# One-hot weights on ScalarE, chunks of other sizes, t added by TensorE for 16 of 18 tiles, and last loads in rows of 4 KB

## The chip, the cores and the metric

One Trainium2 chip, one NeuronCore. The time is the device time of one execution in microseconds (us), and the number that counts is the median of several runs. One execution is also taken with the hardware profiler; its span and its rows are what the sections below read. Engines: TensorE (PE in the profile; PEld is its weight load), VectorE (DVE), ScalarE (ACT), GpSimd (POOL) and SyncE (SP, which here only issues DMAs).

## The reference, cut to what matters

Input x is 1x256x48x48 (2304 tokens of 256 channels), all in float32.

- Layer 0: group norm, then an attention in which the four heads are folded into the tokens (9216 rows of 64), and x is added. This is the large part.
- Layer 1, attention over slices: tokens t are normalised, a softmax `sw` over 64 slices is computed per token, tokens are gathered into slices, 8 heads attend among the 64 slices, and the result is spread back with `sw` and added to t:

```python
denom = jnp.sum(sw, axis=1)[:, None, :, None] + 1e-09
qs = jnp.einsum('bhnd,bns->bhsd', q, sw) / denom      # ks, vs likewise
tok = jnp.einsum('bhst,bhtd->bhsd', attn, vs)
out = jnp.einsum('bhsd,bns->bnhd', tok, sw).reshape(b, n, H * D)
return out @ Wout + bout                               # t = t + this
```

- Layer 1, experts: t is normalised, a gate takes the best 2 of 8 experts for every token, and t gets the weighted sum of `gelu(t @ W1[e]) @ W2[e]` of the two.
- The output is t turned back to 1x256x48x48.

## The kernel before, in words

The tokens lie as 18 tiles of 128 (`NTT = 18`). `t_sb` holds all 18 in SBUF, each with 256 channels and 8 gate logits (`C + E = 264`).

Layer 0's attention runs from the start to about 1235 us in a loop over 18 query blocks by 36 key pairs; the change leaves it alone. Its small steps for layer 1 (`out_proj`, `turn`, `slices`, `gather`) run beside it, so that at its end `sw`, its transposes `swT` and the sums over tokens (`ts_sum`, `den`, `pts`) are ready.

Most engine calls go through the wrappers `pe`, `dve`, `act`, `pool` (class `InOrder`, line 49; its call is line 57, so most groups of the profile have that line). These calls stay in the order in which they are written. Calls on `nc.…` directly may be moved by the scheduler of the language; the gathers and scatters of the experts (lines 1082 and 1142) are such calls on POOL. DMAs marked SPq are issued by SP in its own order.

What follows the attention, in order:

1. **Attention among the slices** (lines 730 to 854, tiles `ph`, `psc`, `pv`, `pa`, `pk`, `pw`, ending with `tw`). One chain of small matmuls and VectorE steps. Between them `busy(n, spin)` issues n matmuls of 128x256 whose output nobody reads.
2. **Tiles** (lines 857 to 905). For each tile TensorE multiplies `swT` by `tw` into a PSUM bank `py` (the two 64-row halves of a transposed tile serve two tiles). For even tiles VectorE adds t from SBUF and takes the statistics (`bn_stats`, `bn_aggr`); for odd tiles TensorE adds t by a matmul with the identity, VectorE takes the statistics from PSUM, and ScalarE copies the sum to `t_sb`. The tiles come in groups of 6, 6, 4 and 2. At the end of a group POOL computes `rstd_t` and `shift`, SP writes `t_d` (the running t in DRAM), and the function `normed` of the group before lets ScalarE write the normalised rows to `tn2` (a ring of two buffers) and SP write them to `tn_d` in DRAM.
3. **Gate and routing** (lines 917 to 991). VectorE finds the two best experts per token (`lg`, `sel`) and the place of each token in its expert's list (`pos`, `slot`). TensorE counts with `pto` and `pin`; ScalarE computes the exponential `e2` and then loads the table of Gelu.
4. **One-hot stage** (lines 995 to 1055). The list of tokens per expert tile comes from one sum of matmuls. For each of the 36 (choice, tile) pairs j, `what[:, j]` holds two rows of 43 numbers (the one-hot `in_tile` times the token number, and times its weight), `in_row[:, j]` a one-hot of 128; TensorE sums `in_row` times `what` over j into `pw`. `in_row` lies on `t_sb`'s memory. The work is done in four chunks of 9, `in_tile` in two of 18, and `find_experts` (between the chunks) gives the expert of each tile:

```python
for k in range(0, K, G):                 # K = 36, G = 9
    ks = slice(k, k + G)
    if k % NTT == 0:
        find_tile(k, NTT)
    dve.tensor_tensor(what[:, ks], in_tile[:, ks, :]..., wkf[:, ks, :]..., ALU.mult)
    dve.tensor_tensor(in_row[:, ks, :], bc(row[:, ks], ...), back..., ALU.is_equal)
    if k == 0:
        find_experts()
```

   Four VectorE instructions read `pw` (`empties`, `slot_t`, `slot_w`), and 14 spins run meanwhile.
5. **Experts** (lines 1057 to 1194). 36 tiles of 128 tokens always, up to 7 more behind tests. A tile's rows come by an indirect DMA from `tn_d` (`xs`, two buffers; the rows of the last seven tiles go to `late_xs`), W1 comes by SP (two buffers), TensorE turns the rows (`pt`), multiplies (`ph`), ScalarE applies Gelu (`hid`), TensorE multiplies by W2 in SBUF (`py`), and POOL scatters with addition into `t_d`.
6. **Tail**, `to_columns` (line 1213). SP loads t from `t_d` in five blocks of up to 512 tokens, TensorE transposes, VectorE copies the first 128 channels from PSUM to `ob` (three buffers) and ScalarE the others, SP writes the output.

Of the kernel before, what the change touches and what calls it, by code (L numbers as in the profile page):

```python
# [9 lines left out]
FP = mybir.dt.float32  # L10
AF = mybir.ActivationFunctionType
# [51 lines left out]
def layers(  # L63
# [430 lines left out]
    def attention():  # L494
# [180 lines left out]
        [P, 256], FP, name="spin"  # L675
    )
    ps_den = sums_done.enter_context(tc.tile_pool(name="ps_den", bufs=1, space=PSUM))
    ps_o = tail.enter_context(tc.tile_pool(name="ps_o", bufs=5, space=PSUM))
    den = ps_den.tile([P, S], FP, name="den")
    pts = ps_den.tile([P, 2, 2 * S], FP, name="pts")  # L680

# [47 lines left out]

    with tc.tile_pool(name="sa", bufs=1) as sa:  # L730
        tw = sa.tile([P, C + E], FP, name="tw")
        with sums_done, tc.tile_pool(name="ps_b", bufs=3, space=PSUM) as ps_b, tc.tile_pool(
            name="ps_sc", bufs=1, space=PSUM
        ) as ps_sc:

# [5 lines left out]
            for m in range(2):  # L741
                for c in range(2):
# [3 lines left out]
                    )  # L746
            busy(1, spin)
            rd = sa.tile([P, S], FP, name="rd")
            dve.tensor_scalar(rd, den, 1e-9, None, ALU.add)
            dve.reciprocal(rd, rd)  # L750
            dr = sa.tile([P, S], FP, name="dr")
            dve.tensor_mul(dr, den, rd)

            def times_dr(b, n):
# [32 lines left out]

            psc = ps_sc.tile([P, 2, 512], FP, name="psc")
            for u in range(2):
# [21 lines left out]
            act.activation(a, a, AF.Exp, scale=float(D1) ** -0.5)  # L811
            act.copy(vs, pv)
            aT = sa.tile([S, 2, 2, P], FP, name="aT")
            for v in range(2):
# [5 lines left out]
                else:  # L820
                    act.copy(aT[:, v], pa)
            busy(1, spin)
            dve.tensor_reduce(am, a, AX.X, ALU.add)
# [46 lines left out]
        shift = const.tile([P, NTT], FP, name="shift")  # L870
        with tc.tile_pool(name="ps_y0", bufs=7, space=PSUM) as ps_y0, tc.tile_pool(
            name="norm", bufs=2
        ) as norm:
            groups = [(0, 6), (6, 6), (12, 4), (16, 2)]
            for g, (i0, n) in enumerate(groups):
                pys = [ps_y0.tile([P, C + E], FP, name="py", tag="py") for _ in range(n)]
                for k, py in enumerate(pys):
                    j, u = divmod(i0 + k, 2)
                    rows = slice(u * S, (u + 1) * S)
                    pe.matmul(py, swT[rows, j, :], tw[rows, :], start=True, stop=(u == 0))  # L880
                for k in range(1, n, 2):
                    pe.matmul(pys[k], ident, t_sb[:, i0 + k, :], start=False, stop=True)
                for k, py in enumerate(pys):
                    i = i0 + k
                    s6 = small.tile([P, 6], FP, name="s6", tag="s6")
                    if k % 2 == 0:
                        dve.tensor_tensor(t_sb[:, i, :], t_sb[:, i, :], py, ALU.add)
                        dve.bn_stats(s6, t_sb[:, i, 0:C])
                    else:
                        dve.bn_stats(s6, py[:, 0:C])  # L890
                        act.copy(t_sb[:, i, :], py)
                    dve.bn_aggr(stats[:, i, :], s6)
                these = slice(i0, i0 + n)
                ve = small.tile([P, n], FP, name="ve6", tag="ve6")
                dve.tensor_scalar(ve, stats[:, these, 1], 1e-5, None, ALU.add)
                pool.tensor_tensor(rstd_t[:, these], ve, mhalf[:, 0:n], ALU.pow)
                pool.tensor_tensor(shift[:, these], stats[:, these, 0], rstd_t[:, these], ALU.mult)
                pool.tensor_scalar(shift[:, these], shift[:, these], -1.0, None, ALU.mult)
                nc.sync.dma_start(
                    out=t_d[i0 * P : (i0 + n) * P, :].rearrange("(i p) c -> p i c", p=P),  # L900
                    in_=t_sb[:, these, 0:C],
                )
                if g > 0:
                    normed(*groups[g - 1])
            normed(*groups[-1])

# [7 lines left out]
    with gating, tc.tile_pool(name="onehot", bufs=1) as oh, tc.tile_pool(  # L914
# [84 lines left out]
        in_tile = oh.tile([P, K, NSL], FP, name="in_tile")  # L999
        what_flat = oh.tile([P, K * 2 * NSL], FP, name="what")  # L1000
        what = what_flat.rearrange("p (k w n) -> p k w n", k=K, w=2)
        in_row = t_flat[:, 0 : K * P].rearrange("p (k r) -> p k r", r=P)
        pwide = ps_lg.tile([P, P], FP, name="pw")
        pw = pwide[:, 0 : 2 * NSL].rearrange("p (w n) -> p w n", w=2)
        busy(7, spin)
        G = 9
        wkf = wk.rearrange("p k i w -> p (k i) w")

        def find_tile(k, n):
# [4 lines left out]
            )  # L1014

        past = gp.tile([1, NSL, E - 1], FP, name="past")

        def find_experts():

            dve.tensor_tensor(  # L1020
                past, bc(steps[0:1, 0:NSL], [1, NSL, E - 1]),
                ends[0:1, 0 : E - 1].unsqueeze(1).to_broadcast([1, NSL, E - 1]), ALU.is_ge,
            )
            ex = gp.tile([1, NSL], FP, name="ex")
            dve.tensor_reduce(ex, past, AX.X, ALU.add)
            dve.tensor_copy(expert_i, ex)
            dve.tensor_copy(used_i, ends[0:1, E - 1 : E])

        for k in range(0, K, G):
            ks = slice(k, k + G)  # L1030
            if k % NTT == 0:
                find_tile(k, NTT)
            dve.tensor_tensor(
                what[:, ks], in_tile[:, ks, :].unsqueeze(2).to_broadcast([P, G, 2, NSL]),
                wkf[:, ks, :].unsqueeze(3).to_broadcast([P, G, 2, NSL]), ALU.mult,
            )
            dve.tensor_tensor(
                in_row[:, ks, :], bc(row[:, ks], [P, G, P]),
                back.unsqueeze(1).to_broadcast([P, G, P]), ALU.is_equal,
            )  # L1040
            if k == 0:
                find_experts()
        for j in range(K):
            n = 2 * NSL if j % G == G - 1 else P
            pe.matmul(
                pwide[:, 0:n], in_row[:, j, :], what_flat[:, j * 2 * NSL : j * 2 * NSL + n],
                start=(j == 0), stop=(j == K - 1),
            )
        busy(14, spin)

# [13 lines left out]
    with tc.tile_pool(name="ps_h", bufs=1, space=PSUM) as ps_h, tc.tile_pool(  # L1064
# [16 lines left out]
        def rows(s, xs):  # L1081
            nc.gpsimd.indirect_dma_start(  # L1082
                out=xs, out_offset=None, in_=tn_d[:, :],
                in_offset=bass.IndirectOffsetOnAxis(ap=slot_t[:, s : s + 1], axis=0),
                bounds_check=NT + P - 1, oob_is_err=True,
            )
            return xs
# [36 lines left out]
        def second(s, hid, meanwhile):  # L1124

            e = expert_of(s, mybir.EngineType.PE)
            py = next(ring_py)
            for f in range(NHC):
                pe.matmul(
                    py, hid[:, f, :],  # L1130
                    w2_sb[:, bass.ds(e, 1), f, :].rearrange("p e d -> p (e d)"),
                    start=(f == 0), stop=(f == NHC - 1),
                )
                if f == 2:
                    meanwhile()
            e = expert_of(s, mybir.EngineType.DVE)
            y = next(ring_y)
            dve.tensor_tensor(
                y, py, b2_e[:, bass.ds(e, 1), :].rearrange("p e d -> p (e d)"), ALU.add
            )  # L1140
            dve.tensor_scalar(y, y, slot_w[:, s : s + 1], None, ALU.mult)
            nc.gpsimd.indirect_dma_start(  # L1142
                out=t_d[:, :], out_offset=bass.IndirectOffsetOnAxis(ap=slot_t[:, s : s + 1], axis=0),
                in_=y, in_offset=None, bounds_check=NT + P - 1, oob_is_err=True,
                compute_op=ALU.add,
            )
# [51 lines left out]
def kernel(ctx: ExitStack, tc: tile.TileContext, *args):  # L1198
# [9 lines left out]

    again = nc.values_load(
        bad, min_val=0, max_val=1, skip_runtime_bounds_check_because="it is the result of a comparison"  # L1210
    )

    def to_columns():

        sp = InOrder(tc, nc.sync)
        with tc.tile_pool(name="fin", bufs=1) as fin, tc.tile_pool(name="fin3", bufs=3) as fin3, tc.tile_pool(
# [3 lines left out]
            for (t0, n), tt in zip(TBLOCKS, tts):  # L1220
                sp.dma_start(out=tt, in_=t_d[t0 : t0 + n, :].rearrange("(i p) c -> p i c", p=P))
            for (t0, n), tt in zip(TBLOCKS, tts):
                ob = fin3.tile([P, 2, 512], FP, name="ob", tag="ob")
                for c in range(2):
                    pt = ps_f.tile([P, 512], FP, name="pt", tag="pt")
                    for k in range(n // P):
                        nc.tensor.transpose(  # L1227
                            pt[:, k * P : (k + 1) * P], tt[:, k, c * P : (c + 1) * P], ident
                        )
                    if c == 0:  # L1230
                        nc.vector.tensor_copy(ob[:, c, 0:n], pt[:, 0:n])  # L1231
                    else:
                        nc.scalar.copy(ob[:, c, 0:n], pt[:, 0:n])  # L1233
                sp.dma_start(out=out_v[:, :, t0 : t0 + n], in_=ob[:, :, 0:n])
# [40 lines left out]
```

## Time and profile before

| | us |
|---|---|
| median of 3 runs | 1622.19 |
| the 3 runs | 1619.83, 1622.56, 1622.19 |
| the profiled execution's own time | 1621.32 |
| its span | 1619.3 |
| attention among the slices, from the sums to `tw` | 1250 to 1261.5 |
| tiles, first product to `lg` times `rstd_t` | 1261.56 to 1279.69 |
| one-hot stage, `in_tile` to the last product | 1289.10 to 1303.1 |
| first gather of rows, first `pt` | 1304.94, 1309.09 |
| last scatter issued, first load of the tail issued | 1596.09, 1600.19 |

Busy shares of the span: PE 97%, PEld 49%, DVE 65%, ACT 50%, POOL 9%. The page cuts the span in 40 slices of 40.5 us and gives the busy share of each in tenths:

```
PE   7999999999999999999999999999999699999995
PEclk9999999999999999999999999999999899999997
DMA  4000000000000000000000000000003756666665
```

PE and the clock granted to it are full nearly everywhere; the slices that differ are the first, the two around 1260 to 1340 us, and the last. In the timeline each row is a start, a duration, the engine, the line, the operation with output and inputs, the number of instructions merged (a float32 matmul gives two), and in brackets how long the engine was idle before and what ended that. A line "L57" is the wrapper's, so one goes by the names of the tiles.

### The profile page before, as it was taken

To read this page: it belongs to the slowest core of one execution; us is meant where nothing else is said; L and a number is where in the kernel's file an instruction comes from. 1 tells how busy PE (TensorE), PEld (TensorE's weight loads), DVE (VectorE), ACT (ScalarE), POOL (GpSimd) and SP (SyncE) were. 2 spreads that over 40 slices of the span, in tenths; PEclk is the share of its full clock that TensorE was granted. 3 is DMA by queue.
4 is the path that set the end of the run, shared out by engine and by line. 5 is a ranking of instruction groups with operands and counts; after the bars stand their busy time and mean duration, and the time that the engine had idled before them with its cause. 6 is when DMAs were issued, how large, how long until landed. Compare 5 with 4: busy or idle time off the path is not lost. (4 is left out here: it accounts for less than half of the span.)

```text
span 1619.3 us, 31854 instructions
## 1 busy us (share of the span) xinstructions
PE 1569.0 (97%) x13230; PEld 786.1 (49%) x13230; DVE 1046.2 (65%) x1369; ACT 810.8 (50%) x1100; POOL 140.3 (9%) x128
## 2 busy tenths in 40 slices
PE   7999999999999999999999999999999699999995
PEld 3633343333333333333333333333335489999995
DVE  7577778777787877877878778778687721111111
ACT  2365555555555655556556555565553322333321
POOL 0000000000000000000000000000000143333321
PEclk9999999999999999999999999999999899999997
DMA  4000000000000000000000000000003756666665
GB/s 137 1 1 1 1 1 1 1 1 1 1 1 1 2 1 1 1 1 2 1 1 1 1 1 1 1 1 1 1 2 98 253 182 189 178 181 190 173 157 181
DMA packets 39910, 79.26 MB, mean 49 GB/s; under 512 B 3613, under 2 KB 26218, under 8 KB 39626
## 3 DMA queue, kind: packets, MB, share of 16 engines
q1 hardware_dynamic: 32074, 66.35, 12.3%
q0 software_dynamic: 7680, 10.75, 3.8%
q8 instruction: 108, 1.77, 0.5%
q14 instruction: 48, 0.39, 0.1%
HBM read 64.64 MB, written 12.45 MB: 48 GB/s over the span
## 5 line engine op out<-in xcount | busy, mean ns | idle before, releaser
L57 DVE TENSOR_TENSOR acc<-acc,p 128x1024 f32<-128x1024 f32 x612 | 748.2, 1222 | 251.6 <-ACT p L57 243.5
L57 ACT ACTIVATE p<-s 128x1024 f32<-128x1024 f32 x648 | 662.9, 1023 | 490.0 <-PE s L57 479.8
L57 PE MATMUL av<-p,v_sb 64*64 64x512 f32 x5184 | 675.4, 590 | 1.0 <-DVE up L57 0.7
L57 PE MATMUL s<-q,kk 64*64 64x512 f32 x5184 | 676.2, 591 | 0.0
L57 PEld LDWEIGHTS s<-q,kk 64*64 64x64 f32 x5184 | 201.6, 133 | 352.6 <-issue 181.7
L57 PEld LDWEIGHTS av<-p,v_sb 64*64 64x64 f32 x5184 | 195.6, 131 | 358.3 <-ACT p L57 202.5
L57 ACT ACTIVATE hid<-ph,bcol 128x128 f32<-128x128 f32 x312 | 89.3, 368 | 216.9 <-PE ph L57 216.2
L57 PE MATMUL py<-w_sb,hid 128*128 x624 | 147.3, 379 | 0.0
L57 PEld LDWEIGHTS ph<-xT,w 128*128 128x128 f32 x1248 | 145.3, 192 | 2.7 <-DVE xT L57 0.8
L57 PE MATMUL ph<-xT,w 128*128 128x128 f32 x1248 | 145.7, 275 | 0.5 <-DVE xT L57 0.5
L57 POOL TENSOR_TENSOR rstd_t<-ve,mhalf 128x1 f32<-128x1 f32 (+3 forms) x22 | 28.0, 1271 | 1234.1 <-DVE ve L57 1234.1
L57 DVE COPY xT<-pt 128x256 f32<-128x256 f32 x40 | 17.0, 425 | 173.3 <-PE pt L57 173.3
L57 PEld LDWEIGHTS py<-w_sb,hid 128*128 128x128 f32 x624 | 112.7, 190 | 12.2
L1142 POOL DMA_INDIRECT t_d<-y,slot_t x39 | 61.7, 1583 | 98.7 <-DVE y L57 86.2
L57 DVE TENSOR_TENSOR y<-py,b_bc 128x256 f32<-128x256 f32 x39 | 16.6, 425 | 68.6 <-PE py L57 68.6
L1082 POOL DMA_INDIRECT xs<-tn_d,slot_t x36 | 38.4, 1065 | 110.6 <-PE pt L57 83.8
L57 DVE RECIPROCAL rinv<-pb 128x256 f32<-128x256 f32 x18 | 31.5, 1751 | 0.0
L57 DVE TENSOR_TENSOR acc<-p 128x1024 f32<-128x1024 f32 x18 | 22.1, 1225 | 9.9 <-ACT p L57 9.9
L314 DVE TENSOR_SCALAR q<-pp,bcol 64x512 f32<-64x512 f32 (+1 forms) x30 | 20.8, 694 | 7.4 <-PE pp L297 7.1
L57 DVE TENSOR_REDUCE up<-av 128x512 f32<-128x1024 f32 x18 | 21.9, 1217 | 0.0
L319 ACT ACTIVATE kk<-pp,bcol 128x512 f32<-128x512 f32 (+1 forms) x10 | 6.4, 644 | 21.8 <-PE pp L301 21.8
L297 PE MATMUL pp<-t_sb,WqT 128*128 128x512 f32 (+1 forms) x40 | 17.2, 553 | 0.0
(260 smaller groups left out, 602.0 us busy)
## 6 DMA issues: line engine op xcount, KB each, us to landing
w<-in_L_ffn_W_dram SPq DMA_DIRECT2D x40, 1024.0 KB, 5.6
w_sb<-in_L_ffn_W_dram SPq DMA_DIRECT2D x8, 1024.0 KB, 13.1
x_sb<-in_x_dram SPq DMA_DIRECT2D x4, 576.0 KB
t<-t_d SPq DMA_DIRECT2D x4, 512.0 KB, 6.9
out_dram<-ob SPq DMA_DIRECT2D x4, 512.0 KB
t_d<-t_sb SPq DMA_DIRECT2D x2, 768.0 KB, 3.6
tn_d<-tn SPq DMA_DIRECT2D x2, 768.0 KB, 3.7
b_bc<-in_L_ffn_b_dram SPq DMA_DIRECT2D x1, 1024.0 KB
```

The lines of the kernel that those rows point to most:

```text
L57: return self.tc.keep_in_program_order(getattr(self.engine, name)(*args, **kwargs))
L297: nc.tensor.matmul(pq[:, 0:tn], WqT[:, c, cols], xn[:, c, toks], start=(c == 0), stop=(c == 1))
L314: nc.vector.tensor_scalar(dst, pq[rows, 0:tn], bcol[rows, B_Q + m : B_Q + m + 1], 0.125, ALU.add, ALU.mult,)
L319: nc.scalar.activation(kk[:, m, toks], pk[:, 0:tn], AF.Identity, bias=bk_m)
L1082: nc.gpsimd.indirect_dma_start(out=xs, out_offset=None, in_=tn_d[:, :], in_offset=bass.IndirectOffsetOnAxis(ap=slot_t[:, s : s + 1], axis= ...
L1142: nc.gpsimd.indirect_dma_start(out=t_d[:, :], out_offset=bass.IndirectOffsetOnAxis(ap=slot_t[:, s : s + 1], axis=0), in_=y, in_offset=None ...
```

## The change

In the slices' attention the two PSUM banks of `den` and `pts` and the two of `psc` are made full banks. As soon as each has been read for the last time, TensorE puts a tile of t there by a matmul with the identity (tiles 0 to 3, in place of two spins); the later product with `tw` adds to it. For the other tiles TensorE adds t after the product, except for tiles 4 and 6, where VectorE still adds. Seven banks are used in turn. Group 0 is normalised after group 1's tiles, the others after all tiles.

```diff
+        def token_sums(i):
+            pe.matmul(banks[i][:, 0 : C + E], ident, t_sb[:, i, :], start=True, stop=False)
...
-            busy(1, spin)
...
+            for i in range(2):
+                token_sums(i)
...
+            token_sums(2)
             aT = sa.tile([S, 2, 2, P], FP, name="aT")
...
-            busy(1, spin)
+            token_sums(3)
...
+            banks = cycle(banks + [ps_y0.tile([P, 512], FP, name=f"py{k}") for k in range(3)])
+            by_dve = (4, 6)
...
+                for i in range(i0, i0 + n, 2):
+                    two = range(i, i + 2)
+                    for u, k in enumerate(two):
+                        rows = slice(u * S, (u + 1) * S)
+                        pe.matmul(
+                            pys[k - i0], swT[rows, i // 2, :], tw[rows, :], start=(k >= 4),
+                            stop=(k < 4 or k in by_dve),
+                        )
+                    for k in two:
+                        if k >= 4 and k not in by_dve:
+                            pe.matmul(pys[k - i0], ident, t_sb[:, k, :], start=False, stop=True)
...
-                    if k % 2 == 0:
+                    if i in by_dve:
...
-                if g > 0:
-                    normed(*groups[g - 1])
-            normed(*groups[-1])
+                if g == 1:
+                    normed(*groups[0])
+            for group in groups[1:]:
+                normed(*group)
```

In the one-hot stage ScalarE computes the weight rows, one instruction for each j; VectorE computes the token rows. The chunks are 3, 6, 9, 9, 6, 3, `in_tile` is made in 9, 9 and 18, and TensorE's products follow each chunk. The experts of the tiles are counted with the tile number on the partitions (7 numbers instead of 301) and turned by TensorE (`pex`). After it 9 spins, not 14.

```diff
+            for j in range(k, k + n):
+                act.activation(what[:, j, 1], in_tile[:, j, :], AF.Copy, scale=wkf[:, j, 1:2])
...
+            past = gp.tile([P, E - 1], FP, name="past")
+            dve.tensor_scalar(past, ends[:, 0 : E - 1], token1[:, 0:1], None, ALU.is_lt)
+            ex = gp.tile([P, 1], FP, name="ex")
+            dve.tensor_reduce(ex, past, AX.X, ALU.add)
+            pex = ps_lg.tile([1, P], FP, name="pex")
+            pe.transpose(pex, ex, ident)
...
+        for n in (3, 6, 9, 9, 6, 3):
+            ks = slice(k, k + n)
+            if k == 9:
+                dve.tensor_copy(expert_i, pex[:, 0:NSL])
+                find_tile(9, 9)
+            elif k == 18:
+                find_tile(18, 18)
+            dve.tensor_tensor(what[:, ks, 0], in_tile[:, ks, :], bc(wkf[:, ks, 0], [P, n, NSL]), ALU.mult)
...
-        busy(14, spin)
+        busy(9, spin)
```

The gathers and scatters of the experts, and the load of the flag `again`, are kept in program order:

```diff
-            nc.gpsimd.indirect_dma_start(
+            pool.indirect_dma_start(
                 out=xs, out_offset=None, in_=tn_d[:, :],
...
-            nc.gpsimd.indirect_dma_start(
+            pool.indirect_dma_start(
                 out=t_d[:, :], out_offset=bass.IndirectOffsetOnAxis(ap=slot_t[:, s : s + 1], axis=0),
...
+    for flag in flags:
+        tc.keep_in_program_order(flag)
```

In the tail a partition loads four consecutive tokens (two in the last block), that is 4 KB in one row instead of four rows of 1 KB. The transposed tokens then come out in another order, and the copies to `ob` restore it by writing with a step of four numbers:

```diff
-                sp.dma_start(out=tt, in_=t_d[t0 : t0 + n, :].rearrange("(i p) c -> p i c", p=P))
+                sp.dma_start(out=tt, in_=t_d[t0 : t0 + n, :].rearrange("(p i) c -> p i c", p=P))
...
+                    dst = ob[:, c, 0:n].rearrange("q (p k) -> q k p", p=P)
+                    src = pt[:, 0:n].rearrange("q (k p) -> q k p", p=P)
                     if c == 0:
-                        nc.vector.tensor_copy(ob[:, c, 0:n], pt[:, 0:n])
+                        nc.vector.tensor_copy(dst, src)
                     else:
-                        nc.scalar.copy(ob[:, c, 0:n], pt[:, 0:n])
+                        nc.scalar.copy(dst, src)
```

## Prediction

> **What bounds the kernel now.** I read the page first. Its line by slices shows TensorE at 97% and DMA idle through the attention, and a stretch near 1240 to 1310 us where TensorE dips. Neither attention nor the expert loop is touched, so I then took the merged timeline of 1241 to 1345 us, the waits of TensorE in the expert loop, and the chain that ended last for the tail. Between `tw` (1261.07) and the first gather of rows (1304.94) TensorE does not set the time: a chain of VectorE, ScalarE and DMA does.
>
> First, the timeline of the tiles: start, duration, engine, operation, and in brackets idle time and its releaser.
> ```profile
> 1261.07 0.43 DVE L57 TENSOR_TENSOR tw<-pw,bout_bc 128x264 f32<-128x264 f32 x1 [1.25 <-PE pw L57]
> ...
> 1265.40 0.40 DVE L57 BATCH_NORM_STATS2 s<-py 128x6 f32<-128x256 f32 x1
> 1265.83 0.38 ACT L57 COPY t_sb<-py 128x264 f32<-128x264 f32 x1 [1.09 <-DVE s L57]
> 1265.84 0.18 DVE L57 BATCH_NORM_AGGREGATE stats<-s 128x2 f32<-128x6 f32 x1
> 1265.93 0.40 DVE L57 TENSOR_TENSOR t_sb<-t_sb,py 128x264 f32<-128x264 f32 x1
> ...
> 1279.69 0.31 DVE L57 TENSOR_TENSOR lg<-lg,rstd_t 128x144 f32<-128x144 f32 x1
> ```
> The reader is to see that a tile summed by TensorE costs VectorE 0.53 us (1265.40 to 1265.93), and that ScalarE's copy starts only when the statistics are read.
>
> Second, the timeline from the norms to the one-hot stage.
> ```profile
> 1283.19 1.09 ACT L57 ACTIVATE tn<-t_sb,shift,rstd_t 128x256 f32<-128x256 f32 x2 [1.80 <-DMA tn_d<-tn]
> ...
> 1284.31 0.36 SPq L865 DMA_DIRECT2D tn_d<-tn  x1
> ...
> 1289.10 0.97 DVE L57 TENSOR_TENSOR in_tile<-first_slot,at_big 128x774 f32<-128x774 f32 x1
> ```
> The last two norms wait for a write of `tn_d`: the ring `tn2` has two buffers.
>
> Third, the timeline from the last one-hot matmuls to the third tile of the experts.
> ```profile
> 1299.53 1.35 DVE L57 TENSOR_TENSOR t_sb<-row,back 128x1152 f32<-128x1152 f32 x1
> 1299.79 3.39 PE L57 MATMUL pw<-what,t_sb 128*128 128x128 f32 x28
> ...
> 1303.01 6.24 PE L57 MATMUL spin<-Wqkv_sb,ident 128*128 128x256 f32 x28
> 1303.21 0.26 DVE L57 TENSOR_SCALAR empties<-pw,spare 128x43 f32<-128x43 f32 x1 [2.33 <-PE pw L57]
> ...
> 1304.94 1.33 POOL L1082 DMA_INDIRECT xs<-tn_d,slot_t  x1 [25.83 <-DVE slot_w L57]
> ...
> 1317.10 1.01 POOL L1082 DMA_INDIRECT xs<-tn_d,slot_t  x1 [0.30 <-issue]
> ...
> 1320.43 0.44 PE L57 MATMUL pt<-ident,xs 128*128 128x128 f32 x2 [1.52 <-DMA xs<-tn_d,slot_t]
> ```
> VectorE ends at 1300.88 and then waits 2.33 for nine matmuls; the third tile's gather is the tenth on POOL's queue, and TensorE idles 1.52 for it. After that TensorE runs through to 1595, so what is won before 1320 is won at the end.
>
> **Step 1, slices' attention: +0.4.** Four additions of t (128x264; six passes took 1.60, so about 0.47 for a sum of two passes) replace two spins (0.45 each, from 14 in 6.24). The first two fill a gap of TensorE (the products with `hsT` start at 1252.67, two sums from 1251.70 end at 1252.65): 0 to 0.1. The third waits for VectorE's last read of `psc` (1256.39) and is queued ahead of `pa`, which started at 1256.96; `pv`'s last passes end near 1256.85, so `pa` slips to about 1257.3: +0.35. The fourth takes a spin's place. Cover gone altogether: +1.0.
>
> **Step 2, the tiles: -2.6.** VectorE now has 16 tiles at 0.53 and two (4 and 6) at 0.99 (add 0.43, statistics 0.56), 10.5 in place of 15.25 (1262.37 to 1277.62). TensorE needs 0.48 for a pair of products and 0.47 for each of 12 sums, 10.0: it keeps up. But the gain is cut. The two halves of `psc` are one tile, and in the built order the statistics of its second half wait for ScalarE's copy of its first (tiles 3, 10, 17). Tile 17's does so behind ScalarE's six norms of group 0 (3.06), which start after copy 11. Counting from the first product: copy 11 ends at 9.4, norms at 12.5, copies 12 to 16 at 13.8, statistics 14.3, copy 17 at 14.7, POOL's `rstd_t` for two tiles (0.72) at 15.4, `lg` times `rstd_t` at 15.5. Before, it stood at 18.1 (1261.56 to 1279.69). Bounds: 13 without those waits, 17 if ScalarE's norms take 0.59 each. With step 1, `lg` stands 2.2 earlier.
>
> **Step 3, the floor: gives back 0.6.** ScalarE now runs norms 1 to 3 only after copy 17: group 1 ends at 17.8, SP (which now issues `t_d` of groups 2 and 3 first) writes it, 3.7 to 4.1 to landing; only then, at 21.6, the last two norms (1.09), and behind them in ScalarE's queue `e` (the exponential), then the table load (1.28). `e` is done at 23.0, that is near 1285.0, no earlier than now; VectorE would want it at 1284.7. And `in_tile`, whose memory is that of `tn2`, waits for the last write of `tn_d`: issued at 1284.7, 2.8 to landing, 1287.5. So the one-hot stage starts at 1287.5 in place of 1289.10: -1.6 net of steps 1 to 3 (-1.2 with 4.1). What is late next is this write, not VectorE.
>
> **Step 4, one-hot stage: -1.4.** Before: 1289.10 to the matmuls' end at 1303.1, 14.0. VectorE drops from 9252 to 7704 elements a partition (1.04 ns each, some 0.07 to 0.19 per instruction by the spacing of those rows): about 10.0 to the end. TensorE's 36 products cost 0.245 (18 passes in 2.21); the chunks of 9 at 5.4 and 8.2 pile up, and from 8.2 the last 18 run back to back: 12.6. ScalarE's 36 weights have no row. Below: 0.19, the gelu spacing (four in 1.14 with one of 0.37: 0.257) less 85 elements at 0.85 ns; above: 0.51, the norms' spacing. I take 0.20, since the 128x18 exponential (0.22 long) and the 128x128 gelu frame the size. The last 18 start at 6.3 and end at 9.9, ahead of TensorE; they begin to pace at 0.34. At 0.51 the stage ends at 15.8. `expert_i` comes near 1290.9 (1293.39 before), so the first W1 loads stay hidden.
>
> **Step 5, spins: -0.4.** After the last product there are 9 spins (4.0) for 14 (6.24). Before, `pt` started the moment the spins ended, 5.8 after the products; the gather (1.83 after them, some 3.3 to 3.7 to landing) allows 5.1 to 5.5.
>
> **Step 6, POOL's order: -1.3.** The gathers are now kept in program order: the third tile's is eighth, not tenth, 2 x 1.315 earlier; it lands about 0.6 ahead of TensorE's need. Bounds 0 (the W1 load then holds the DMA engines; one gather here took 6.6) to -1.5.
>
> **Step 7, the tail: -0.1.** The windows of the tail and of a W1 load, columns: us, length, busy of five engines, granted clock, DMA share, GB/s.
> ```profile
> 1604.00:1606.00 2.00, 1.73 (x8) 1.57 (x8) 0.43 (x1) 0.00 (x0) 0.00 (x0) 0.50 1.09 370
> ...
> 1612.00:1614.00 2.00, 0.00 (x0) 0.00 (x0) 0.42 (x1) 0.37 (x1) 0.00 (x0) 0.78 0.92 336
> ```
> DMA is full while the tail reads 2.36 MB in rows of 1 KB at 370 GB/s; W1, in rows of 4 KB, came at 418 to 434 in its full half microseconds (1296.5 to 1300). That is 6.4 against 5.6: up to -0.7. Against it, the ten copies to `ob` now write with a step of 16 bytes. The row nearest to that is `both` (0.40 where its equals take 0.31, a step of 72 bytes): 0.63 ns an element, 0.32 a copy. Two of each pair are in series and the last blocks wait for `ob` buffers, so 0 to +0.8. I take half of each: about -0.5 and +0.4.
>
> Two rules bear on it. The Trainium skill, "SBUF — State Buffer", section "Door 1: The DMA port swizzle", says that successive accesses run at full speed inside a 16-byte line and pay on each crossing; here every element crosses, so by it the copies lose their share in full and the tail is +0.3. "DMA: Bandwidth & Descriptors", "Why small descriptors are slow (HBM only)", has about 3 cycles lost per packet and merging worthwhile only to 256 bytes; an estimate by it (35/32 against 131/128) gives 0.4, not 0.7, for the rows of 4 KB.
>
> **Sum.** -1.6 - 1.4 - 0.4 - 1.3 - 0.1 = -4.8. The profiled execution took 1621.32 (span 1619.3): 1616.5. It lies 0.9 under the median 1622.19, which would give 1617.4; I forecast **1617.0**.
>
> **Rivals.**
> (a) ScalarE becomes the bound of the one-hot stage (spacing of 0.4 to 0.51) or the third gather still stalls: 1.6 to 3.2 given back, -1.6 to -3.2, 1618.9 to 1620.6, within 0.2%. For it: each product waits for a ScalarE weight. Against: every short ScalarE row.
> (b) The tail's rows pay in full and strides are free, no slip in step 1: -5.9, 1616.
> (c) Slower: TensorE's clock. It fell to 0.50 some 2.6 us after its last work (1272.74 to 1275.3) and came back only after 4.0 us of spins (1288.7). If a smaller chunk or fewer spins leave a gap over 2.6 us after warming, the 36 products run at 0.49: +7 to +9, and +2 to +4 over the whole, 1624 to 1626. My gaps are at most 1.2, so this decides only if the weights or the gather come 1.4 late.
> (d) The change does not do what it says: the floor of step 3 eats step 2 wholly, and steps 4 to 6 remain: -3.1, 1619.
>
> **Numbers.** A measurement of this kernel can tell about 0.2% (3.2 us). Forecast 0.60 (faster), (b) 0.10 (faster), (a) 0.15 and (d) 0.09 (within), (c) 0.06. Range: from 1614.2 (own time less 6.1, every bound at its best, less 0.9 for the spread of the runs shown) to 1620.8 (the end of (a)); it leaves out (c) and extremes, some 0.15.
>
> **What would show it.** Right: `in_tile` near 1287.5 waiting for a DMA; last two norms still held by `tn_d`; products ending 12.6 after `in_tile`; no wait of TensorE for `xs`; `ob` copies above 0.69 and 0.59. Wrong: weights further apart than 0.34, a granted clock of 0.5 beyond 1290, or a floor that moved.

## The result, and the profile after

The changed kernel took **1616.37 us** (median of 7 runs, 1615.14 to 1616.80) against 1622.13 for the kernel before beside it (7 runs, 1619.83 to 1622.56): ratio 0.9966, 95% interval 0.9956 to 0.9976. The profiled execution has a span of 1614.3, 5.0 less than before. Stage by stage, in the two profiled executions (us):

| stage | before | after | change | forecast |
|---|---|---|---|---|
| first `ph` of the slices' attention to `tw` (step 1) | 10.34 | 10.86 | +0.52 | +0.4 |
| first product of the tiles to `lg` times `rstd_t` (2) | 18.13 | 15.40 | -2.73 | -2.6 |
| `lg` times `rstd_t` to `in_tile` (3) | 9.41 | 9.40 | 0 | +0.6 |
| `in_tile` to `empties` (4) | 14.11 | 12.54 | -1.57 | -1.4 |
| `empties` to the first `pt` (5) | 5.88 | 4.90 | -0.98 | -0.4 |
| first `pt` to the third tile's `pt` (6) | 11.34 | 10.69 | -0.65 | -1.3 |
| third `pt` to the last scatter | 275.66 | 275.65 | 0 | 0 |
| last scatter to the end of the span (7) | 23.19 | 22.74 | -0.45 | -0.1 |

The sum is -5.9. The span shows only 5.0, because after's execution reached the first `ph` 0.93 later (1251.66 for 1250.73), in code that the change does not touch. Over all profiled executions here that time lies anywhere from 1250.73 to 1251.67.

The tiles, in the timeline of after (start, duration, engine, operation, idle time and its releaser):
```profile
1262.52 0.43 DVE L57 TENSOR_TENSOR tw<-pw,bout_bc 128x264 f32<-128x264 f32 x1 [1.25 <-PE pw L57]
...
1264.32 0.40 DVE L57 BATCH_NORM_STATS2 s<-pts 128x6 f32<-128x256 f32 x1
...
1272.18 3.06 ACT L57 ACTIVATE tn<-t_sb,shift,rstd_t 128x256 f32<-128x256 f32 x6
...
1276.22 0.39 ACT L57 COPY t_sb<-psc 128x264 f32<-128x264 f32 x1
...
1276.64 0.43 DVE L57 BATCH_NORM_STATS2 s<-psc 128x6 f32<-128x256 f32 x1 [0.63 <-ACT t_sb L57]
...
1278.41 0.31 DVE L57 TENSOR_TENSOR lg<-lg,rstd_t 128x144 f32<-128x144 f32 x1 [0.22 <-POOL rstd_t L57]
```
A tile summed by TensorE costs VectorE only its statistics, read straight from PSUM (1264.32). The last of them are held by ScalarE's copy of the other half of `psc`, which itself stood behind the six norms of group 0 (1272.18); that is the limit which step 2 named. Next the norms and the one-hot stage, same view:
```profile
1284.28 1.09 ACT L57 ACTIVATE tn<-t_sb,shift,rstd_t 128x256 f32<-128x256 f32 x2 [1.88 <-DMA tn_d<-tn]
...
1287.64 0.20 DVE L57 SCALAR_TENSOR_TENSOR row<-first_slot,slot 128x36 f32<-128x36 f32 x1
1287.81 0.56 DVE L57 TENSOR_TENSOR in_tile<-first_slot,at_big 128x387 f32<-128x387 f32 x1
...
1294.11 4.09 ACT L57 ACTIVATE what<-in_tile,wk 128x43 f32<-128x43 f32 x18 [0.64 <-DVE in_tile L57]
1294.59 1.35 DVE L57 TENSOR_TENSOR t_sb<-row,back 128x1152 f32<-128x1152 f32 x1
...
1296.09 4.22 PE L57 MATMUL pw<-what,t_sb 128*128 128x128 f32 x36 [0.53 <-ACT what L57]
...
1297.27 0.55 DVE L57 TENSOR_TENSOR t_sb<-row,back 128x384 f32<-128x384 f32 x1
...
1300.35 0.26 DVE L57 TENSOR_SCALAR empties<-pw,spare 128x43 f32<-128x43 f32 x1 [2.53 <-PE pw L57]
```
The last two norms still wait for a write of `tn_d`, but `in_tile` follows `row` with no wait: it waits for no write. ScalarE makes a weight every 0.227 us (18 in 4.09), TensorE a product every 0.234 (36 passes in 4.22), and VectorE is done 2.5 us before `empties` can start. The gathers and the first tiles:
```profile
1302.07 1.33 POOL L57 DMA_INDIRECT xs<-tn_d,slot_t  x1 [22.92 <-DVE slot_w L57]
...
1305.25 0.44 PE L57 MATMUL pt<-ident,xs 128*128 128x128 f32 x2 [1.02 <-DMA xs<-tn_d,slot_t]
...
1311.62 1.01 POOL L57 DMA_INDIRECT xs<-tn_d,slot_t  x1 [0.30 <-issue]
...
1315.94 0.44 PE L57 MATMUL pt<-ident,xs 128*128 128x128 f32 x2 [0.81 <-DMA xs<-tn_d,slot_t]
```
The first `pt` now waits for its gather and no longer for the spins; the third tile's wait fell from 1.52 to 0.81 and did not go.

### The profile page after: what moved, and what is told of

It reads as the page before. It is cut to its first block, busy times and chain, and to the rows that moved or that the text cites. A ratio compares the mean times of both kernels' runs of the same rounds, so it can differ in the third digit from the quotient of the medians.

```text
span 1614.3 us, 31899 instructions
## 1 busy us (share of the span) xinstructions
PE 1569.7 (97%) x13231; PEld 786.4 (49%) x13231; DVE 1043.5 (65%) x1367; ACT 824.0 (51%) x1143; POOL 140.7 (9%) x128
## 5 line engine op out<-in xcount | busy, mean ns | idle before, releaser
L297 PE MATMUL pp<-t_sb,WqT 128*128 128x512 f32 (+1 forms) x40 | 17.6, 562 | 0.0
```

The source lines that it names most:

```text
L297: nc.tensor.matmul(pq[:, 0:tn], WqT[:, c, cols], xn[:, c, toks], start=(c == 0), stop=(c == 1))
```

## The experiments

Three groups ran on three chips, each group beside its own runs of the kernel before. On the chips of the second and third group VectorE and ScalarE stood still in the second tile (last experiment below); times compare within a group, stages outside that place compare across all.

| kernel | group | median (runs) | before | ratio, 95% interval |
|---|---|---|---|---|
| tail_old_rows | 1 | 1616.47 (6) | 1621.65 | 0.9968, 0.9956 to 0.9980 |
| tail_read_step | 1 | 1616.14 (5) | 1621.65 | 0.9962, 0.9948 to 0.9976 |
| tail_pe_step | 1 | 1615.58 (5) | 1621.65 | 0.9960, 0.9946 to 0.9973 |
| third_buffer | 1 | 1615.07 (5) | 1621.65 | 0.9957, 0.9943 to 0.9971 |
| spins_14 | 2 | 1622.24 (8) | 1625.22 | 0.9977, 0.9967 to 0.9988 |
| weights_by_vector | 2 | 1622.19 (11) | 1625.22 | 0.9979, 0.9970 to 0.9988 |
| chunks_of_9 | 2 | 1623.04 (11) | 1625.22 | 0.9981, 0.9972 to 0.9990 |
| norm_ring_4 | 2 | 1620.28 (5) | 1625.22 | 0.9963, 0.9950 to 0.9977 |
| after_again | 3 | 1619.98 (6) | 1625.16 | 0.9967, 0.9955 to 0.9979 |
| before_again | 3 | 1626.50 (11) | 1625.16 | 0.9998, 0.9989 to 1.0007 |
| spins_14_again | 3 | 1622.60 (11) | 1625.16 | 0.9979, 0.9970 to 0.9988 |
| three_mends | 3 | 1619.07 (5) | 1625.16 | 0.9959, 0.9945 to 0.9972 |

An interval of 0.0025 is 4 us wide, so edits worth a microsecond are read from the stages of the profile, which repeat within 0.1 us outside the standstill and the tail.

**Does the write of `tn_d` hold the one-hot stage (step 3)?**
```diff
-            name="norm", bufs=2
+            name="norm", bufs=4
```


> The changed kernel with four tn2 buffers, so that no norm waits for a write of tn_d (the last two wait 1.88 now). Step 3 of the forecast (this write sets when in_tile starts and gives back 0.6): in_tile starts 9.4 less 0.6 after lg times rstd_t, so 8.8, total -0.6. What the trace of after says (VectorE's own chain sets it, in_tile follows row directly): 9.4 as now, total within 0.3.

Its timeline:
```profile
1277.16 6.01 ACT L57 ACTIVATE tn<-t_sb,shift,rstd_t 128x256 f32<-128x256 f32 x12
...
1278.19 0.31 DVE L57 TENSOR_TENSOR lg<-lg,rstd_t 128x144 f32<-128x144 f32 x1 [0.22 <-POOL rstd_t L57]
...
1283.09 0.22 ACT L57 ACTIVATE e<-e 128x18 f32<-128x18 f32 x1
...
1285.38 0.16 DVE L57 TENSOR_SCALAR w1st<-e 128x18 f32<-128x18 f32 x1
...
1287.61 0.56 DVE L57 TENSOR_TENSOR in_tile<-first_slot,at_big 128x387 f32<-128x387 f32 x1
```
All twelve norms now run without a wait and `e` is done at 1283.31, 2.1 us before VectorE asks for it. Yet `in_tile` starts 9.42 after `lg` times `rstd_t` (1278.19), as it did with two buffers (9.40). The write set nothing; VectorE's own chain did. In after the last write is issued at 1285.4, and its transfer has left the DMA engines by 1287.2, 0.6 before `in_tile`: the margin is thin, and so is that of `e`, which ends at 1285.48 for a use at 1285.59.

**What makes the one-hot stage shorter (step 4)?**
```diff
-            for j in range(k, k + n):
-                act.activation(what[:, j, 1], in_tile[:, j, :], AF.Copy, scale=wkf[:, j, 1:2])
...
-            dve.tensor_tensor(what[:, ks, 0], in_tile[:, ks, :], bc(wkf[:, ks, 0], [P, n, NSL]), ALU.mult)
+            dve.tensor_tensor(
+                what[:, ks], in_tile[:, ks, :].unsqueeze(2).to_broadcast([P, n, 2, NSL]),
+                wkf[:, ks, :].unsqueeze(3).to_broadcast([P, n, 2, NSL]), ALU.mult,
+            )
```


> The changed kernel with both rows of the one-hot weights by VectorE (as before), chunks kept. VectorE has 1548 more elements a partition, some 1.6 us. If VectorE paces the stage (step 4): in_tile to the products' end 12.4 now, 13.6 to 14.0 then. If TensorE's 36 products pace its end: VectorE ends at 11.6, three products after it, 12.5 to 12.9. The compiled order has the third gather seventh, so the third tile's 0.81 stall should be gone: the total +1.2 by the first, -0.3 by the second.


```diff
-        for n in (3, 6, 9, 9, 6, 3):
+        for n in (9, 9, 9, 9):
```


> The changed kernel with chunks of 9, 9, 9, 9 in place of 3, 6, 9, 9, 6, 3; the weights stay with ScalarE. If the smaller chunks bring the gain of step 4: in_tile to the products' end 13 or more (12.4 now). If VectorE's lighter load does, and TensorE's products pile up in either case: VectorE ends at 9.9, nine products of 0.245 after it, 12.1 to 12.5. The third gather is seventh in the compiled order, so the stall of 0.81 should be gone: the total -0.6 to -1.0 by the second.

The timeline of weights_by_vector, where `in_tile` starts at 1287.68:
```profile
1295.67 1.35 DVE L57 TENSOR_TENSOR t_sb<-row,back 128x1152 f32<-128x1152 f32 x1
...
1297.07 4.25 PE L57 MATMUL pw<-what,t_sb 128*128 128x128 f32 x36 [0.90 <-DVE t_sb L57]
...
1298.75 0.55 DVE L57 TENSOR_TENSOR t_sb<-row,back 128x384 f32<-128x384 f32 x1
...
1301.36 0.26 DVE L57 TENSOR_SCALAR empties<-pw,spare 128x43 f32<-128x43 f32 x1 [2.06 <-PE pw L57]
```
And that of chunks_of_9, from 1287.12:
```profile
1294.15 1.35 DVE L57 TENSOR_TENSOR t_sb<-row,back 128x1152 f32<-128x1152 f32 x1
...
1295.65 4.22 PE L57 MATMUL pw<-what,t_sb 128*128 128x128 f32 x36 [0.53 <-ACT what L57]
...
1299.91 0.26 DVE L57 TENSOR_SCALAR empties<-pw,spare 128x43 f32<-128x43 f32 x1 [2.66 <-PE pw L57]
```
From `in_tile` to `empties` the two take 13.68 and 12.79; after takes 12.54. So of the 1.57 won, 1.14 belong to the weights on ScalarE and 0.25 to the smaller chunks, each undone alone. The other 0.2 is not tested: the shorter count of the experts, which held VectorE for 1.13 before (1292.25 to 1293.38) and 0.50 after, was not undone.

Neither expectation had the mechanism whole. With the weights on VectorE the products end 13.64 after `in_tile`, the size that the first alternative gave, and VectorE ends at 11.62, as worked out, but the stage does not end three products later. The last 18 products run back to back in 4.2 us in all three kernels, and what counts is when they start: 8.28 after `in_tile` in after, 9.39 with the weights on VectorE, 8.53 with chunks of 9. With the weights on VectorE that is 0.05 after VectorE ends the row block of the chunk that begins at the 19th product. In the other two it is 0.15 after it, and the profile names a weight from ScalarE as what they waited for, so the weights cost about 0.1 there. What VectorE does after that row block lies beside TensorE.

The totals of the two are not explained by this: they lie 1.9 and 2.8 above norm_ring_4 in the same group, the stage 1.1 and 0.25 above. Where the rest comes from is not shown: the profiled executions differ by only 0.7 and 0.8 in span, and 0.2 and 0.9 of that stand between the first and the third `pt`, in the standstill, which also hides the third gather (seventh in all three).

**Spins and POOL's queue (steps 5 and 6).**
```diff
-        busy(9, spin)
+        busy(14, spin)
```


> The changed kernel with 14 spins after the one-hot products, not 9; in the compiled order that alone puts the third tile's gather back to tenth on POOL's queue, though it is issued through the same pinned object. Steps 5 and 6 undone, then. Theory (step 6's order follows from the spins, not from the pinning): first pt 5.8 after the products' end (5.0 now), third pt with a stall of 1.5 or more, so the total +1.7 to +2.6. Step 5 alone would be +0.4 to +0.9; if the third tile shows no more than the 0.81 stall of now, the place in the queue was worth nothing.

> spins_14 once more beside its control, since the standstill covered the third tile there. Theory: first pt 5.87 after empties (4.90 in the control), and where no standstill covers it, a wait of 1.5 or more for the third gather, tenth in POOL's queue; total 1.7 to 2.6 above the control. If the queue place costs nothing beyond the stall of 0.81 that the control has: +0.9.


```diff
-        ring_xs, ring_w1 = ring(fp, 2, [P, C], "xs"), ring(fp, 2, [P, 2, HID], "w1")
+        ring_xs, ring_w1 = ring(fp, 3, [P, C], "xs"), ring(fp, 2, [P, 2, HID], "w1")
```


> The changed kernel with three xs buffers, not two: the third tile's gather becomes third on POOL's queue (eighth now) and waits for no transpose. Theory (the 0.81 stall of the third tile's transposes is the place in POOL's queue): the stall goes, third pt 0.8 earlier against the first pt (10.69 after it now, 9.9 then), total -0.8. Rival (the gather is slow because W1 holds the DMA engines, or W1 itself is late next): a wait for xs or w1 of 0.5 or more stays, total within 0.3 of the changed kernel.

With 14 spins the first `pt` stood 5.87 and 5.88 after `empties` (9 spins: 4.85 to 4.96 in all ten executions), which is all of step 5's stage, 0.98. The third tile could not be read in either run: the standstill lay over it, and `pt` there shows no wait for `xs`. In the third group the total is 2.6 above the control (1622.60 for 1619.98), the upper end of what was expected, but how much of it is the queue stays open.

The traces show where the order does not come from. With 14 spins the third tile's gather is tenth on POOL, issued directly (before) or through the pinned object (spins_14 and its repeat). With 9 spins, pinned, it is eighth, and seventh in norm_ring_4 and in the two kernels of step 4. So the pinning alone moved nothing, and fewer spins did. No run has 9 spins without the pinning, and why the scheduler of the language puts the gather forward is not shown; that it reckons TensorE free sooner is a guess.

third_buffer, on a chip without the standstill, shows what an early gather is worth:
```profile
1304.49 1.01 POOL L57 DMA_INDIRECT xs<-tn_d,slot_t  x1 [0.30 <-issue]
...
1304.66 0.44 PE L57 MATMUL pt<-ident,xs 128*128 128x128 f32 x2 [0.97 <-DMA xs<-tn_d,slot_t]
...
1314.38 0.38 PE L57 MATMUL pt<-ident,xs 128*128 128x128 f32 x2
```
Gathered third, the third tile's rows are there in time, and its `pt` stands 9.72 after the first, for 10.63 to 10.72 in the four other executions of the changed code without a standstill. The total agrees (1615.07, the lowest of its group), as far as the intervals can tell.

The DMA packets show why eighth was not early enough. In after, W1's load was issued at 1310.07 and its packets moved from 1311.14 to 1314.68; the gather, issued at 1311.62, moved its first packet at 1314.31, 2.7 later. In before the gather came at 1317.10, near the end of W1's packets (1315.05 to 1318.84), and moved 1.2 later; in third_buffer, at 1304.49 and ahead of that load, 0.4 later. This is the bound of 0 that step 6 named (W1's load holds the DMA engines). No run moved that load alone.

**The tail (step 7).**
```diff
-                sp.dma_start(out=tt, in_=t_d[t0 : t0 + n, :].rearrange("(p i) c -> p i c", p=P))
+                sp.dma_start(out=tt, in_=t_d[t0 : t0 + n, :].rearrange("(i p) c -> p i c", p=P))
...
-                        nc.vector.tensor_copy(dst, src)
+                        nc.vector.tensor_copy(ob[:, c, 0:n], pt[:, 0:n])
...
-                        nc.scalar.copy(dst, src)
+                        nc.scalar.copy(ob[:, c, 0:n], pt[:, 0:n])
```


> The changed kernel, but with the last loads of t_d in rows of 1 KB and unstrided copies to ob, as before. Measured from the start of the last scatter to the end of the span: 19.11 us before, 18.63 after. Theory (the rows of 4 KB pay more than the strided copies cost): 19.0 to 19.2, copies 0.69 and 0.59, the total 0.3 to 0.6 above the changed kernel. Step 7 as forecast: 18.7, total +0.1. Rival (the strided copies cost more than the rows bring, and the 0.48 seen is drift between runs): 18.2 to 18.5, total lower.

The two lengths in that text (19.11 and 18.63) are counted from the first load of the tail, not from the scatter; so are the lengths here.
```diff
-                    dst = ob[:, c, 0:n].rearrange("q (p k) -> q k p", p=P)
-                    src = pt[:, 0:n].rearrange("q (k p) -> q k p", p=P)
+                    dst = ob[:, c, 0:n].rearrange("q (p k) -> q p k", p=P)
+                    src = pt[:, 0:n].rearrange("q (k p) -> q p k", p=P)
```


> The changed kernel with rows of 4 KB, but the ten copies walk ob in order and step through PSUM (512 bytes) instead of writing with a step of 16 bytes. Theory A (a write step is what costs): copies back at 0.69 (VectorE) and 0.59 (ScalarE), tail 17.8 to 18.4. Theory B (any step costs, on either side): copies 1.07 and 1.09 or above, tail 18.6 or more.


```diff
-                            pt[:, k * P : (k + 1) * P], tt[:, k, c * P : (c + 1) * P], ident
+                            pt[:, 0:n].rearrange("q (p k) -> q k p", p=P)[:, k, :], tt[:, k, c * P : (c + 1) * P], ident
```
(and plain copies, as in tail_old_rows)

> The changed kernel with rows of 4 KB, but TensorE's transposes write PSUM with a step of 16 bytes and the copies are plain. Theory A (the cost lies in VectorE's and ScalarE's access): copies 0.69 and 0.59, transposes as now (36 in 6.71), tail 17.8 to 18.4. Theory B (a stepped write costs TensorE too): 36 transposes in 8 us or more, tail 18.6 or more.

First transposes and first copies in the timeline of after, then of tail_read_step and of tail_pe_step:
```profile
1599.43 6.71 PE L1252 MATMUL pt<-ident,t 128*128 128x128 f32 x36 [8.97 <-DMA t<-t_d]
1600.73 1.07 DVE L1259 COPY ob<-pt 128x512 f32<-128x512 f32 x1 [9.42 <-PE pt L1252]
1601.45 1.09 ACT L1261 COPY ob<-pt 128x512 f32<-128x512 f32 x1 [13.42 <-DMA t<-t_d]
```
```profile
1599.85 7.00 PE L1252 MATMUL pt<-ident,t 128*128 128x128 f32 x36 [9.78 <-DMA t<-t_d]
1601.15 0.69 DVE L1259 COPY ob<-pt 128x512 f32<-128x512 f32 x1 [10.23 <-PE pt L1252]
1601.87 0.59 ACT L1261 COPY ob<-pt 128x512 f32<-128x512 f32 x1 [14.24 <-DMA t<-t_d]
```
```profile
1599.14 5.93 PE L1252 MATMUL pt<-ident,t 128*128 128x128 f32 x36 [8.93 <-DMA t<-t_d]
1600.44 0.69 DVE L1259 COPY ob<-pt 128x512 f32<-128x512 f32 x1 [9.38 <-PE pt L1252]
1601.16 0.59 ACT L1261 COPY ob<-pt 128x512 f32<-128x512 f32 x1 [13.38 <-DVE ob L1259]
```
Writing with a step of 16 bytes costs the copies 0.38 and 0.50; stepping through PSUM on the read side costs nothing. TensorE's stepped write into PSUM costs nothing either: its transposes follow each other every 0.21 us at a granted clock of 0.50 and every 0.11 at 1.00, as the plain ones do. The tail in all profiled executions (us):

| tail | executions | first load to first transpose | first transpose to the end | first load to the end |
|---|---|---|---|---|
| rows of 1 KB, plain copies | 3 | 4.08 to 4.30, mean 4.16 | 14.93 to 15.09, mean 15.01 | 19.09 to 19.23, mean 19.17 |
| rows of 4 KB, stepped copies (after) | 8 | 3.57 to 3.85, mean 3.69 | 14.89 to 15.75, mean 15.27 | 18.66 to 19.46, mean 18.96 |
| rows of 4 KB, TensorE steps | 2 | 3.75, 3.70 | 14.40, 14.58 | 18.15, 18.28 |
| rows of 4 KB, copies step through PSUM | 1 | 4.53 | 14.84 | 19.37 |

Up to the first transpose the rows bring 0.47. Behind it, later loads, copies and output run together, so rows and copies are told apart only over the whole tail. Rows of 4 KB without stepped copies (TensorE steps) bring 1.0 (18.21 for 19.17). The stepped copies take 0.75 of it back (18.96), and step 7 is worth -0.2; the 0.45 in the table of stages is its lucky side. Between 7 and 8 us after the first load the DMA engines are busy for 0.72 in after, for 0.98 in tail_pe_step: with stepped copies they run short of work there. The two executions with TensorE's step lie below all eight of after, but they are only two. tail_read_step does not fit: its copies are fast, but its first block landed late, the only one of eleven with rows of 4 KB to do so, and its total says nothing.

**The slip in the slices' attention (step 1), and the three mends together.** Besides the third `xs` buffer and TensorE's step in the tail:
```diff
-            token_sums(2)
             aT = sa.tile([S, 2, 2, P], FP, name="aT")
...
-            token_sums(3)
+            token_sums(2)
...
-            busy(1, spin)
+            token_sums(3)
             tok_sb = sa.tile([P, 4, D1], FP, name="tok_sb")
```


> The changed kernel with three edits together: three xs buffers; the tail's transposes writing with a step of 16 bytes, copies plain; the third token sum after pa and the fourth in place of the spin behind pk. Expected against the control: first ph to tw 10.4 (10.86), third pt 0.9 earlier against the first, from the last scatter to the end 0.5 shorter: -1.9 in all, some 1614.3 where the control has 1616.4. If one gain is taken back by the next wait, -1.0 or less.

From its timeline:
```profile
1256.87 0.42 ACT L57 ACTIVATE a<-a 128x256 f32<-128x256 f32 x1 [5.81 <-DVE a L57]
1257.34 0.63 PE L57 MATMUL pa<-ident,a 128*64 128x128 f32 x4
```
`pa` starts 0.05 after `a` (in after, 1258.43 for `a` ended at 1257.84: 0.59), and `ph` to `tw` is 10.36, the length of before: step 1's 0.5 was the third sum ahead of `pa`, whole (the fourth moved too, but `pa` no longer waits). From the last scatter to the end it is 0.4 shorter (22.46 for 22.85 in the control). What the third buffer brings cannot be read beside the standstill (first to third `pt` 15.66, in the control 14.27). The medians differ by 0.9 (1619.07 for 1619.98), what two of the three mends should give, but the intervals overlap and do not prove it. It is the best version that ran beside the control; on a chip without the standstill it was not tried.

**The standstill.**

> The changed kernel itself, as a control on the chip of this group. In spins_14, weights_by_vector, chunks_of_9 and norm_ring_4 VectorE and ScalarE stood still between 1309 and 1315 us (xT of the second tile 8.2 to 8.9 after the first, 4.6 in the runs of the other group), and no edit of theirs comes near. If that belongs to the chip, and not to the edits, it appears here too when the control runs on that chip (first pt to third pt 13 to 16, total near 1620), and not on another (10.7, total 1616). If it belongs to the edits, it is absent on either.

> The kernel before, as a control with a profile. If the standstill of VectorE and ScalarE belongs to the chip, it holds the kernel before as well (first pt to third pt 14 or more where it was 11.34, total near 1625 on that chip), and the ratio of after to before stays near 0.9966. If it is the change that brings it, before shows 11.34 on every chip.

The waits around the second tile, in the timeline of before_again:
```profile
1314.34 0.38 PE L57 MATMUL pt<-ident,xs 128*128 128x128 f32 x2
...
1318.74 1.14 ACT L57 ACTIVATE hid<-ph,bcol 128x128 f32<-128x128 f32 x4 [4.63 <-remote]
...
1320.19 0.42 DVE L57 COPY xT<-pt 128x256 f32<-128x256 f32 x1 [9.58 <-remote]
```
and of after_again:
```profile
1309.88 0.38 PE L57 MATMUL pt<-ident,xs 128*128 128x128 f32 x2
...
1312.31 1.14 ACT L57 ACTIVATE hid<-ph,bcol 128x128 f32<-128x128 f32 x4 [2.88 <-remote]
...
1313.73 0.42 DVE L57 COPY xT<-pt 128x256 f32<-128x256 f32 x1 [7.58 <-remote]
```
`xT` needs only `pt`, and in the execution shown first it followed it at 1310.30; here it comes 5.85 and 3.85 after the transposes start. The kernel before has it too, so the change does not bring it. It goes with the chip: it is in all eight profiled executions of the second and third group and in none of the six others. It varies: ScalarE goes on 2.4 to 3.1 after the second `pt` starts in the five executions whose third gather is early in POOL's queue, 4.4 to 5.9 in the three that have it tenth. Whether the queue place is the cause, and what "remote" stands for, stays open. Part of its price goes with TensorE's clock: while TensorE stood idle, the granted clock fell to 0.50 for 3.4 us in five of the eight executions (third `pt` 14.3 to 16.0 after the first), for 6.8 in before_again and spins_14_again (17.6 and 17.1), and not at all in spins_14 (13.2).

## Why the prediction was right, point by point

The time (1616.37 for a forecast of 1617.0) and all signs but that of step 3 were right. The sum, -4.8, was 1.1 short in the profiled pair: the floor did not hold (0.6), the spins were worth more (0.6), the tail came out well (0.35), the tiles (0.1) and the one-hot stage (0.2) gave a little more; POOL's order gave less (0.65) and step 1 cost 0.1 more. By the mean of the tail's executions (-0.2) the surplus is 0.8. Steps 1, 2 and 4 were right in mechanism and, within 0.2, in size. That the total came so close is in part luck: the misses of steps 3 and 5 and that of step 6 have opposite signs, and within step 7 two terms were both too small and cancel.

- **Step 1** held: the slip of `pa` was 0.5 for 0.35, and moving the third sum takes it back.
- **Step 2** held, with its mechanism: 15.40 for 15.5, tile 17's statistics waiting 0.63 for ScalarE's copy.
- **Step 3 failed.** "What is late next is this write, not VectorE" was wrong. The forecast put the last norms 21.6 after the first product and the landing 2.8 after the write's issue; the norms came at 21.27 and the write was over in 1.8. The trace of before could have told: its last write of the same size, issued at 1284.31, had left the DMA engines by 1286.09, 1.8 later. norm_ring_4 shows that removing every wait of the norms moves `in_tile` by 0.02: what sets it is VectorE's own chain from `lg` to `row`, 9.40 long before and after. Rival (d), this floor grown, falls with it.
- **Step 4** held in size (-1.57 for -1.4) and in its end, the last 18 products back to back. ScalarE's spacing was 0.227 for the 0.20 taken. Rival (a), ScalarE as the bound at 0.4 or more, is out in that part, but barely: the weights were forecast to pace from 0.34 on, and at 0.227 the last 18 products already wait some 0.1 for one.
- **Step 5** was mis-sized: -0.98 for -0.4. From the gather's issue to the first `pt` it took 3.18, below the 3.3 to 3.7 assumed. TensorE now waits for the gather for 1.02 after the spins' end, so by this row fewer spins than 9 would bring nothing more.
- **Step 6**: -0.65 for -1.3, and its cause was wrong. The order moved because of the spins, not the pinning; and eighth was not early enough: the gather took 4.3 from its issue to its use, for 3.3 before, with W1's load ahead of it on the DMA engines (387 GB/s from 1312 to 1314). The prediction had this as its bound of 0. It came true by half, and so did the second part of rival (a), the third gather still stalling.
- **Step 7**: -0.2 for -0.1, by luck. Both halves were about twice what was taken, as far as two executions with TensorE's step tell, and cancel: the rows -1.0 for -0.5, the copies +0.75 for +0.4. The stepped copies themselves cost 0.38 and 0.50, more than the bound of 0.32. The Trainium skill, "SBUF — State Buffer", section "Door 1: The DMA port swizzle", has a penalty for each access that crosses to a new 16-byte line; the copies agree, and the tail loses nearly the full +0.8 of the forecast's bound. The +0.3 that the forecast drew from it did not come, because the rows brought more. For the rows, the estimate of 0.4 by the Trainium skill, "DMA: Bandwidth & Descriptors", section "Why small descriptors are slow (HBM only)", is near the 0.47 up to the first transpose and below the 1.0 of the whole tail; the 0.7 from W1 is nearer to that.
- **Rival (b)**, -5.9 and 1616, is nearer in number than the forecast (stages -5.9, time 1616.37), but not in cause: the stepped copies cost time and step 1 slipped. The 0.6 that step 3 did not give back and the 0.6 more of step 5 made up for it.
- **Rival (c)**, the cold clock, did not come: the granted clock was at 1.00 from 1286.7, and the products took 0.234 each. But its 2.6 us are no fixed delay: over the 14 profiled executions the clock fell 2.45 to 5.0 us after TensorE's last work on the tiles, and came back 0.75 to 4.5 us before the first one-hot product. The margin was thin in some.

## What to carry to other kernels

Where two engines' chains meet within half a microsecond, neither is worth shortening alone: find which one the meeting instruction really waits for, from the row just before it, and count from there. In a pipeline of chunks, what counts is the moment from which the last engine can run without a pause, not the moment at which its supplier ends. Where one edit has a gain and a price, as the rows and the copies here, a sum that comes out right shows neither: run each without the other. A queue's order can hang on an unrelated filler: look at the compiled order after each edit, and give the transfer that is needed early a buffer of its own, which fixed here what a pinned order did not.

## What the runs showed of the hardware

- A 128x512 copy from PSUM to SBUF in fp32 with a 16-byte step on the written side took 1.07 us on VectorE and 1.09 on ScalarE, for 0.69 and 0.59 plain. A 512-byte step on the read side took 0.69 and 0.59, and TensorE's transposes written into PSUM with a 16-byte step were no slower (one every 0.21 us at a granted clock of 0.50 and every 0.11 at 1.00, both ways).
- ScalarE's 128x43 activations with a scale per partition follow each other every 0.22 us (18 in 4.09), though one alone is shown 0.31 to 0.33 long.
- Between the tiles and the one-hot stage, with TensorE idle for 8 to 12 us, the granted clock stayed at 0.50 for 6.83, 10.24 or 13.65 us in the 14 executions, and in the standstill for 3.41 or 6.83: whole multiples of 3.41.
- On two of the chips, VectorE and ScalarE stood still at one place of the program, in the kernel before as in the changed one (third `pt` 13.2 to 17.6 after the first, for 9.7 to 11.3 elsewhere); medians there lie 3 to 4 us higher (before: 1625.2 for 1621.7). A stage table from one chip would have put this on an edit.
